# Seven products of quarters for the second layer of the late slots in a gated cross-attention and mixture-of-experts kernel

## The chip, the core and the metric

The kernel runs on one core of one Trainium2 chip. The metric is the device time of one execution in microseconds. Everything is float32.

## The reference

Four sequences of 1024 tokens with 256 features pass through a gated cross-attention block (16 heads, 64 context tokens for each sequence), and then through a gated feed-forward block of eight experts, of which each token takes two. Cut to what matters here:

```python
x = x + tanh(g_xattn[0]) * xattn(layernorm(x), ctx, ...)

def ffn(x, gate_w, w1, w2):              # x: the layer-normed tokens
    logits = einsum('td,ed->te', xt, gate_w)
    w_topk, sel = top_k(logits, 2)       # 2 of 8 experts, softmax over the two
    combine = zeros(T, E).at[arange(T)[:, None], sel].add(softmax(w_topk))
    h = silu(einsum('td,edf->tef', xt, w1))     # first layer,  256 -> 1024
    y = einsum('tef,efd->ted', h, w2)           # second layer, 1024 -> 256
    return einsum('ted,te->td', y, combine)

x = x + tanh(g_ffn[0]) * ffn(layernorm(x), ...)
```

The kernel doesn't compute all eight experts for each token. It sorts (token, expert) pairs by expert and multiplies only those.

## The kernel before

**Attention** runs over eight groups of 512 tokens. Its parts (queries, scores at L385, softmax, `attend`, `project`) are issued in an order written out by hand in the loop over `g`. While it runs, the routing of the finished groups is worked out on VectorE (`route`, `place`), and lists of (token, weight) pairs are written to memory.

**Slots.** The expert layers run over slots. A slot is one expert and 256 places of its list, in two blocks of 128 tokens. There are 9 early slots (`NA`), taken from the first half of the tokens, and late slots from `s = NA` on. The first seven late slots (9 to 15, `NW`) are wide: they have a third block of 128 tokens. The next five (16 to 20, `NH`) have a third block of 64 tokens. The others (21 to 27) are short and have two blocks. Slot 27 (`s = NA + OFTEN - 1`) is the last that always runs; more slots lie behind a branch.

For each slot:

- `load_ids` and `load_weights` load the list entries and the expert's w1 and w2 on SP's queue, three slots ahead.
- `gather_tokens` fetches the normed tokens with GpSimd's indirect DMAs (L845); `transposed` transposes them on TensorE (L867), and ScalarE copies them out of PSUM.
- `hidden` is the first layer: TensorE at L899, and ScalarE's Silu out of PSUM into `hT` at L907.
- `combine` is the second layer. It gathers the tokens' present outputs into `acc` (GpSimd, L922). For each block `t` it multiplies `hT` by `w2` over 8 tiles of the hidden dimension (TensorE, L978: the stationary operand is a 128x128 tile of `hT`, the moving one 256 columns of w2). Then `add(t)` follows: VectorE takes the product out of PSUM, times each token's weight (L966), into `y` (the tile that held the gathered tokens), GpSimd adds `y` to `acc` (L970), and a scatter writes `acc` back (L939).

`run_slots` puts `combine(s)` behind `hidden(s + 1)` and the transposes of slot `s + 2`, so that TensorE always has work while the other engines finish. Only at the end does the combine of slot 26 follow directly on that of slot 25, ahead of `hidden(27)`. A gather into `acc` waits for the scatters of the slot before it, since both go over the same rows of the output.

**Buffers.** PSUM: the pool `ps1` has four banks, which queries, transposes, and the second layer share in the order in which they come free; the hidden layer has the pool `ps2`. `hT` has two buffers in the share `hidden`, or lies in `group`. The tag `pr` (two buffers) and the tag `nT` (four) are large tiles of the attention phase; in the late slots, `nT` also holds the transposed tokens of wide slots.

The scheduler of the language orders the instructions of each engine; `keep_in_program_order` and `issue_after` pin some of them. Each engine runs its own instructions in that order.

Of the kernel before, what the change touches and what calls it, by code (L numbers as in the profile page):

```python
# [8 lines left out]
F32 = mybir.dt.float32  # L9
I32 = mybir.dt.int32  # L10
AF = mybir.ActivationFunctionType
ALU = mybir.AluOpType
# [3 lines left out]
P = 128  # L16
# [5 lines left out]
def kernel(  # L22
# [13 lines left out]
    w2: bass.AP,  # L36
    out: bass.AP,
):

# [21 lines left out]
    nc = tc.nc  # L61

    B, L, D = x.shape
    M = context.shape[1]
    H, _, DK = w_qs.shape
    E, _, F = w1.shape
# [8 lines left out]
    NF = F // P  # L75
# [5 lines left out]
    NA = -(-(2 * HG * G - E * (S - 1)) // S)  # L81
# [4 lines left out]
    OFTEN, RARELY = 19, 20  # L86
# [27 lines left out]
    of = out.rearrange("b l d -> (b l) d").rearrange("(g t p) d -> g p t d", p=P, t=T)  # L114
# [14 lines left out]
    nT = {}  # L129
# [104 lines left out]
    def apart(tensor, dma, part=None, behind=()):  # L234

        writers = [writer for name in behind for writer in written[name]]
        tc.declare_no_dep(dma.ins, group=tensor, keep=writers, reason="different rows")
        tc.add_to_no_dep_group(tensor, dma.ins)
        for writer in writers:
            tc.add_manual_dep(  # L240
                dma.ins,
                writer.name,
                mybir.DependencyInfo(mybir.DependencyClass.Sync, mybir.DependencyReason.DATA),
                reason="rows of the part",
            )
        if part:
            written.setdefault(part, []).append(dma.ins)
# [133 lines left out]
    def probabilities(g, t, qT):  # L381

        sc = ps2.tile([P, NP // 2, 2, 2, M], F32, tag="ps2", name=f"sc_{g}_{t}")
        for p in range(NP):
            nc.tensor.matmul(  # L385
                sc[:, p // 2, :, p % 2, :],
                of_pair(qT, p)[:, t * P : (t + 1) * P],
                kT[g // GB][:, p, :],
                start=True,
                stop=True,  # L390
            )
        scv = sc.rearrange("p q r j m -> p (q r j) m")
        mx = small.tile([P, H], F32, tag="mx", name=f"mx_{g}_{t}")
        nc.vector.tensor_reduce(mx, scv, AX.X, ALU.max)  # L394
        pr = soft.tile([P, H, M], F32, tag="pr", name=f"pr_{g}_{t}")
        nc.vector.tensor_tensor(  # L396
            pr, scv, mx.unsqueeze(2).to_broadcast([P, H, M]), ALU.subtract
        )
        nc.scalar.activation(pr, pr, AF.Exp)  # L399
        sm = small.tile([P, H], F32, tag="sm", name=f"sm_{g}_{t}")  # L400
        nc.vector.tensor_reduce(sm, pr, AX.X, ALU.add)  # L401
        nc.vector.reciprocal(sm, sm)  # L402
        newest[:] = [
            nc.gpsimd.tensor_tensor(pr, pr, sm.unsqueeze(2).to_broadcast([P, H, M]), ALU.mult).ins  # L404
        ]
        return pr
# [352 lines left out]
    half = len(tiles) // 2  # L759
# [77 lines left out]
    def behind_softmax():  # L837

        return tc.issue_after(newest[0]) if newest else nullcontext()
# [71 lines left out]
    evicted = {}  # L911

    def combine(s, ids, b, y, acc, hT):

        blocks = blocks_of(s)
        n = tokens_of(s)
        behind = [f"slot{s - 1}"] if s else ["out0"]
        if s == NA:
            behind.append("out1")
        for t, r in enumerate(blocks):  # L920
            with behind_softmax():
                gather = nc.gpsimd.indirect_dma_start(  # L922
                    out=acc[t][:r],
                    out_offset=None,
                    in_=outf[:n],
                    in_offset=bass.IndirectOffsetOnAxis(ap=ids[:r, t, 0:1], axis=0),
                    bounds_check=n - 1,
                    oob_is_err=False,
                )
            apart("out", gather, behind=behind)  # L930
        if attention_ends:
            py = [bank(f"py_{s}_{t}")[:, : D * r // P] for t, r in enumerate(blocks)]
        else:
            both = bank(f"py_{s}").rearrange("p (t d) -> p t d", d=D)
            py = [both[:, t, :] for t in range(blocks)]

        def scatter(t):
            r = blocks[t]
            put = nc.gpsimd.indirect_dma_start(  # L939
                out=outf[:n],  # L940
                out_offset=bass.IndirectOffsetOnAxis(ap=ids[:r, t, 0:1], axis=0),
                in_=acc[t][:r],
                in_offset=None,
                bounds_check=n - 1,
                oob_is_err=False,
            )
            apart("out", put, f"slot{s}")

        def parts_of(r):

            return [(slice(i * r, (i + 1) * r), slice(i * D * r // P, (i + 1) * D * r // P)) for i in range(P // r)]

        def add(t):
            r = blocks[t]
            last = s == NA + OFTEN - 1 and t == len(blocks) - 1
            if last:
                tc.keep_in_program_order(
                    nc.vector.scalar_tensor_tensor(
                        acc[t], py[t], ids.bitcast(F32)[:, t, 1:2], acc[t], ALU.mult, ALU.add
                    )  # L960
                )
                scatter(t)
                return

            for rows, columns in parts_of(r):
                evicted[s] = nc.vector.tensor_scalar(  # L966
                    y[t][:r, columns], py[t][rows], ids.bitcast(F32)[rows, t, 1:2], None, ALU.mult
                ).ins
            with behind_softmax():
                nc.gpsimd.tensor_tensor(acc[t][:r], acc[t][:r], y[t][:r], ALU.add)  # L970
                scatter(t)

        each = attention_ends
        per_tile = NF // len(hT)
        for t, r in enumerate(blocks):
            for f in range(NF):
                for rows, columns in parts_of(r):
                    nc.tensor.matmul(  # L978
                        py[t][rows],
                        hT[f // per_tile][:, f % per_tile, t * P : t * P + r],  # L980
                        b[:, f, columns],
                        start=(f == 0),
                        stop=(f == NF - 1),
                    )
            if each:
                add(t)
            yield
        if not each:
            for t in range(len(blocks)):
                add(t)  # L990
# [3 lines left out]
    def run_slots(slots):  # L994
# [28 lines left out]
        for s in slots:  # L1023
            gather(s + ahead)
            a, b = weights.pop(s)
            xin, acc = tokens.pop(s)
            if s == slots[-1] and pending:
                yield from combine(*pending)
                pending = None
            for hT in hidden(s, a, xT):  # L1030
                yield
            if s + 1 in slots:
                xT = transposed(s + 1, tokens[s + 1][0])
                yield
# [74 lines left out]
    for g in range(NG + 3):  # L1109
# [9 lines left out]
        for t in range(T):  # L1119
            if g < NG:  # L1120
                pr = probabilities(g, t, qT)
# [93 lines left out]
```

## Time and profile before

| | |
|---|---|
| median of 3 runs | 889.73 us (889.43 to 890.48) |
| profiled execution, own time | 918.12 us |
| its span, first to last instruction | 916.3 us, mean granted TensorE clock 0.986 |
| TensorE matmuls (PE) busy | 871.4 us (95%) |
| weight loads (PEld) busy | 657.5 us (72%) |
| VectorE (DVE) busy | 327.8 us (36%) |
| ScalarE (ACT) busy | 263.9 us (29%) |
| GpSimd (POOL) busy | 403.0 us (44%) |
| second layer, L978: busy, share of the chain that ended last | 238.3 us, 23% |

The profile is of one execution, whose own time is longer than the median of the runs without a profile. A row of the groups' view has the line, the engine, the operation, out <- in by the program's names, partitions x elements, the count, the busy time, the mean time of one, and the idle time before. Matmul records overlap: the next starts before the last has left the array, so that the distance between starts is the cost, and not the mean duration. Each float32 matmul in the code leaves two matmul records and two weight loads. In the timeline a row merges equal instructions that follow each other: start, length, engine, line, operation and count.

### The profile page before, as it was taken

How to read it: one execution, taken by the hardware profiler on the slowest of the kernel's cores; microseconds unless marked ns; L12 is line 12 of the kernel's file. 1: busy time of each engine (PE TensorE's matmuls, PEld its weight loads, DVE VectorE, ACT ScalarE, POOL GpSimd, SP SyncE). 2: the span in 40 equal slices, each digit the busy share in tenths (PEclk: the TensorE clock that was granted, in tenths of full speed). 3: DMA queues.
4: the chain of work that ended last, by engine and by line, in shares of the span. 5: the costliest groups of instructions: out<-in, count | busy, mean ns of one | idle time of the engine just before them, and what ended most of it. 6: DMA issues, size and time to landing. Idle time of an engine off the chain costs nothing.

```text
span 916.3 us, 11723 instructions
## 1 busy us (share of the span) xinstructions
PE 871.4 (95%) x4328; PEld 657.5 (72%) x4328; DVE 327.8 (36%) x729; ACT 263.9 (29%) x414; POOL 403.0 (44%) x392
## 2 busy tenths in 40 slices
PE   8999999999999998997997899999999999999995
PEld 5556858574857576865885787777777777888884
DVE  3467585777468748631155300000000001100010
ACT  4653353425242425432140121211211211121110
POOL 2051212146213553065447565555455555564443
PEclk9999999999999999998998899999999999999998
DMA  9600000001010225276372575744444564457111
GB/s 203 195 1 1 24 24 24 24 19 30 1 46 1 47 90 188 72 141 143 115 262 63 143 248 166 237 149 140 148 140 142 176 198 148 135 188 267 51 36 42
DMA packets 85279, 102.33 MB, mean 112 GB/s; under 512 B 29366, under 2 KB 71740, under 8 KB 85216
## 3 DMA queue, kind: packets, MB, share of 16 engines
q1 hardware_dynamic: 62656, 66.96, 24.4%
q0 software_dynamic: 11600, 25.25, 8.8%
q10 hardware_dynamic: 10960, 9.31, 3.7%
q8 instruction: 36, 0.59, 0.3%
q14 instruction: 27, 0.22, 0.1%
HBM read 84.75 MB, written 17.33 MB: 111 GB/s over the span
## 4 chain that ended last, share of the span: by engine, by line
PE 80%; DVE 10%; another core or an unknown queue 3%; issue 3%; DMA 1%; POOL 1%; ACT 1%; POOLq 0%; ACTq 0%; DVEq 0%
PE py L978 23%; PE ph L899 22%; PE pp L445 11%; PE pq L370 10%; PE sc L385 5%; PE pa L414 2%; PE pt L867 2%; PE po L428 2%; DVE qT L437 1%; PE pk L317 1%; DVE sm L401 1%; DVE pr L396 1%; DVE mx L394 1%; PE pt_b L281 1%
## 5 line engine op out<-in xcount | busy, mean ns | idle before, releaser
L978 PE MATMUL py<-w,hT 128*128 128x256 f32 (+1 forms) x1168 | 238.3, 369 | 9.2 <-issue 8.7
L899 PE MATMUL ph<-xT,w 128*128 128x256 f32 (+2 forms) x896 | 233.8, 418 | 2.1 <-ACT xT L872 1.2
L978 PEld LDWEIGHTS py<-w,hT 128*128 128x128 f32 (+1 forms) x1168 | 199.8, 184 | 40.2 <-issue 14.0
L899 PEld LDWEIGHTS ph<-xT,w 128*128 128x128 f32 x896 | 170.0, 191 | 57.5 <-issue 1.6
L907 ACT ACTIVATE hT<-ph 128x1024 f32<-128x1024 f32 (+3 forms) x84 | 69.9, 835 | 370.6 <-PE ph L899 319.5
L966 DVE TENSOR_SCALAR x<-py,ids 128x256 f32<-128x256 f32 (+1 forms) x72 | 33.5, 465 | 381.9 <-PE py L978 348.3
L404 POOL TENSOR_TENSOR pr<-pr,sm 128x1024 f32<-128x1024 f32 x32 | 60.9, 1902 | 218.1 <-DVE sm L402 202.1
L370 PE MATMUL pq<-nT_a,wq 128*128 128x512 f32 x256 | 117.0, 597 | 0.4 <-issue 0.2
L445 PE MATMUL pp<-wp,qT 128*128 128x256 f32 x512 | 113.2, 379 | 0.0
L445 PEld LDWEIGHTS pp<-wp,qT 128*128 128x128 f32 x512 | 97.0, 190 | 18.2 <-issue 5.3
L922 POOL DMA_INDIRECT x<-out_dram,ids x68 | 69.3, 1018 | 81.7 <-DMA out_dram<-x,ids 61.9
L845 POOL DMA_INDIRECT x<-normed,ids x68 | 67.9, 999 | 53.4 <-DMA ids<-lists 34.3
L970 POOL TENSOR_TENSOR x<-x,x 128x256 f32<-128x256 f32 (+1 forms) x67 | 48.3, 721 | 90.5 <-DVE x L966 77.8
L370 PEld LDWEIGHTS pq<-nT_a,wq 128*128 128x128 f32 x256 | 45.9, 190 | 53.5 <-issue 47.6
L939 POOL DMA_INDIRECT out_dram<-x,ids x68 | 69.0, 1015 | 23.2 <-POOL x L970 18.0
L568 POOL DMA_INDIRECT lists<-entry,to_row x64 | 62.1, 971 | 20.5 <-issue 17.9
L385 PEld LDWEIGHTS sc<-keys,qT 128*128 128x128 f32 x512 | 62.9, 192 | 7.9 <-issue 7.5
L385 PE MATMUL sc<-keys,qT 128*128 128x128 f32 x512 | 67.4, 278 | 0.0
L415 ACT COPY aT<-pa 128x512 f32<-128x512 f32 x64 | 34.6, 590 | 91.2 <-PE pa L414 71.1
L394 DVE TENSOR_REDUCE mx<-sc 128x16 f32<-128x1024 f32 x32 | 39.0, 1220 | 29.5 <-PE sc L385 28.3
L401 DVE TENSOR_REDUCE sm<-pr 128x16 f32<-128x1024 f32 x32 | 38.9, 1215 | 20.9 <-ACT pr L399 20.9
L377 ACT COPY qT<-pq 128x512 f32<-128x512 f32 x64 | 35.7, 582 | 28.4 <-PE pq L370 28.4
(209 smaller groups left out, 624.8 us busy)
## 6 DMA issues: line engine op xcount, KB each, us to landing
w<-in_L_ffn_w_dram SPq DMA_DIRECT2D x56, 1024.0 KB
out_dram<-x ACTq DMA_DIRECT2D x8, 512.0 KB
normed<-keep_b ACTq DMA_DIRECT2D x8, 512.0 KB
x<-in_x_dram SPq DMA_DIRECT2D x7, 512.0 KB
x<-normed,ids POOLq DMA_INDIRECT x68
x<-out_dram,ids POOLq DMA_INDIRECT x68
out_dram<-x,ids POOLq DMA_INDIRECT x68
wq<-in_L_xattn_w_qs_dram SPq DMA_DIRECT2D x4, 256.0 KB
```

The costliest lines, as they stand in the source:

```text
L370: nc.tensor.matmul(pq, wq[:, c, p * P : (p + 1) * P], nT[g][:, c, :], start=(c == 0), stop=(c == NC - 1),)
L385: nc.tensor.matmul(sc[:, p // 2, :, p % 2, :], of_pair(qT, p)[:, t * P : (t + 1) * P], kT[g // GB][:, p, :], start=True, stop=True,)
L404: nc.gpsimd.tensor_tensor(pr, pr, sm.unsqueeze(2).to_broadcast([P, H, M]), ALU.mult).ins
L445: nc.tensor.matmul(pp[:, i, :], of_pair(qT, p)[:, t * P : (t + 1) * P], wp[:, p, :], start=(p == 0), stop=(p == NP - 1),)
L568: nc.gpsimd.indirect_dma_start(out=lists, out_offset=bass.IndirectOffsetOnAxis(ap=to_row[:, k, i : i + 1], axis=0), in_=entry[:, k, i, :], ...
L845: gather = nc.gpsimd.indirect_dma_start(out=xin[t][:n], out_offset=None, in_=normed[: tokens_of(s)], in_offset=bass.IndirectOffsetOnAxis(a ...
L899: nc.tensor.matmul(ph[:, i, :], a[:, c, f * P : (f + 1) * P], xT[:, c, :], start=(c == 0), stop=(c == NC - 1),)
L907: nc.scalar.activation(hT[f0 // per_tile][:, f1 : f1 + step, :], ph, AF.Silu)
L922: gather = nc.gpsimd.indirect_dma_start(out=acc[t][:r], out_offset=None, in_=outf[:n], in_offset=bass.IndirectOffsetOnAxis(ap=ids[:r, t, 0 ...
L939: put = nc.gpsimd.indirect_dma_start(out=outf[:n], out_offset=bass.IndirectOffsetOnAxis(ap=ids[:r, t, 0:1], axis=0), in_=acc[t][:r], in_of ...
L970: nc.gpsimd.tensor_tensor(acc[t][:r], acc[t][:r], y[t][:r], ALU.add)
L978: nc.tensor.matmul(py[t][rows], hT[f // per_tile][:, f % per_tile, t * P : t * P + r], b[:, f, columns], start=(f == 0), stop=(f == NF - 1),)
```

## The change

For the late slots 9 to 26, the second layer of the two whole blocks is computed as one matrix product of 256 tokens x 1024 hidden by 1024 hidden x 256 outputs, cut in the middle along all three. That makes four quarters of `hT`, four of `w2` and four of the output. The output's quarters come from seven products of quarters (in place of eight), of which five use sums of quarters:

- `quarters()` lets VectorE form eight sums of 128 partitions x 512 elements: s1 to s4 of `hT`'s quarters and t1 to t4 of `w2`'s. s3 is written over a quarter of `hT` and t1 over a quarter of `w2`; the others go to tiles of the tags `pr` and `nT`.
- `seven_products()` has TensorE multiply 128x128 tiles, four for each product, each product into a PSUM bank of its own. ScalarE takes product 1 out twice (once for each block's weights, into `partial`), and VectorE adds each of the others to the quarters of `y` in which it takes part, times the token's weight: eight `scalar_tensor_tensor` of 128x128. `finish(i)` is the add to `acc` and the scatter of block `i`.
- A third block, where there is one, is multiplied as before, but now ahead of the two whole blocks. Its `add`, which VectorE begins by taking it out of PSUM, is issued behind `quarters()`.

The early slots, slot 27 and the slots behind the branch stay as they are.

In the built program the scheduler moves some of VectorE's sums: s1 of the next slot stands among the additions of the slot before, and t3 (in short slots t1 too) of the next slot ahead of them. t1, t2 and t4 of wide slots stand directly ahead of the third block's leave from PSUM; in slots with a half block the leave's two halves stand on either side of t4. On GpSimd, the third block's add and scatter go ahead of those of the two whole blocks. ScalarE gets two more instructions a slot, and SP's order is unchanged.

```diff
+        whole = 2 if NA <= s < NA + OFTEN - 1 else 0
         if attention_ends:
-            py = [bank(f"py_{s}_{t}")[:, : D * r // P] for t, r in enumerate(blocks)]
+            py = [bank(f"py_{s}_{t}")[:, : D * r // P] if t >= whole else None for t, r in enumerate(blocks)]
...
+        def quarters():
...
+            s1, s2, s3, s4 = sums[:, 0], sums[:, 1], h[1][0], rest[:, 0]
+            t1, t2, t3, t4 = w[0][1], more[:, 0], rest[:, 1], more[:, 1]
+            for to, one, sign, other in (
+                (s1, h[1][0], ALU.add, h[1][1]),
+                (s3, h[0][0], ALU.subtract, h[1][0]),
+                (s2, s1, ALU.subtract, h[0][0]),
+                (s4, h[0][1], ALU.subtract, s2),
+                (t3, w[1][1], ALU.subtract, w[0][1]),
+                (t1, w[0][1], ALU.subtract, w[0][0]),
+                (t2, w[1][1], ALU.subtract, t1),
+                (t4, w[1][0], ALU.subtract, t2),
+            ):
+                nc.vector.tensor_tensor(to, one, other, sign)
+            return h, w, (s1, s2, s3, s4), (t1, t2, t3, t4)
+
+        def seven_products(h, w, hsums, wsums):
...
+            def product(name, left, right):
+                to = bank(f"py_{s}_{name}")[:, :P]
+                n = NF // 2
+                for f in range(n):
+                    nc.tensor.matmul(to, left[:, f, :], right[:, f, :], start=(f == 0), stop=(f == n - 1))
+                return to
...
+            def plus(to, of, i, sofar):
+                evicted[s] = nc.vector.scalar_tensor_tensor(to, of, weight[i], sofar, ALU.mult, ALU.add).ins
+
+            p = product("1", h[0][0], w[0][0])
+            for i in range(2):
+                nc.scalar.activation(partial[:, i], p, AF.Copy, scale=weight[i])
+            p = product("2", h[0][1], w[1][0])
+            plus(own[0], p, 0, partial[:, 0])
+            fifth = product("5", s1, t1)
+            plus(own[1], fifth, 0, partial[:, 0])
+            p = product("7", s3, t3)
+            plus(own[2], p, 1, partial[:, 1])
+            p = product("6", s2, t2)
+            plus(own[1], p, 0, own[1])
+            plus(own[2], p, 1, own[2])
+            plus(own[3], fifth, 1, own[2])
+            p = product("3", s4, w[1][1])
+            plus(own[1], p, 0, own[1])
+            finish(0)
+            p = product("4", h[1][1], t4)
+            plus(own[2], p, 1, own[2])
+            finish(1)
+
+        def finish(i):
+            with behind_softmax():
+                nc.gpsimd.tensor_tensor(acc[i], acc[i], y[i], ALU.add)
+                scatter(i)
+
         each = attention_ends
         per_tile = NF // len(hT)
         for t, r in enumerate(blocks):
+            if t < whole:
+                continue
             for f in range(NF):
...
-            if each:
+            if each and not whole:
                 add(t)
             yield
+        if whole:
+            operands = quarters()
+            for t in range(whole, len(blocks)):
+                add(t)
+            seven_products(*operands)
+            yield
```

More of the change, by code (lines that the diff above doesn't have):

```diff
@@ L971, in add @@
                 scatter(t)
+        def quarters():
+            half = NF // 2
+            if len(hT) == 2:
+                h = [[hT[k][:, :, i * P : (i + 1) * P] for k in range(2)] for i in range(2)]
+            else:
+                h = [
+                    [hT[0][:, k * half : (k + 1) * half, i * P : (i + 1) * P] for k in range(2)]
+                    for i in range(2)
+                ]
+            w = [[b[:, k * half : (k + 1) * half, j * P : (j + 1) * P] for j in range(2)] for k in range(2)]
+            sums, more = (
+                soft.tile([P, 2, half, P], F32, tag="pr", name=f"{kind}_{s}") for kind in ("hsum", "wsum")
+            )
+            rest = npool.tile([P, 2, half, P], F32, tag="nT", name=f"rest_{s}")
+            s1, s2, s3, s4 = sums[:, 0], sums[:, 1], h[1][0], rest[:, 0]
[12 more added lines that the diff above has]
+            return h, w, (s1, s2, s3, s4), (t1, t2, t3, t4)
@@ new lines, in seven_products @@
+        def seven_products(h, w, hsums, wsums):
+            s1, s2, s3, s4 = hsums
+            t1, t2, t3, t4 = wsums
+            weight = [ids.bitcast(F32)[:, i, 1:2] for i in range(2)]
+            def product(name, left, right):
[4 more added lines that the diff above has]
+                return to
+            partial = work.tile([P, 2, P], F32, tag="xn", name=f"partial_{s}")
+            own = [y[i][:, j * P : (j + 1) * P] for i in range(2) for j in range(2)]
+            def plus(to, of, i, sofar):
[19 more added lines that the diff above has]
+            finish(1)
```

## The prediction

> **What bounds the kernel now.** I read the page first: span, shares, the 40 slices and the granted clock.
>
> ```profile
> span 916.3 us, 11723 instructions
> PE 871.4 (95%) x4328; PEld 657.5 (72%) x4328; DVE 327.8 (36%) x729; ACT 263.9 (29%) x414; POOL 403.0 (44%) x392
> ...
> PE   8999999999999998997997899999999999999995
> ...
> DVE  3467585777468748631155300000000001100010
> ...
> PEclk9999999999999999998998899999999999999998
> ```
>
> TensorE (PE) is full in nearly every slice. From slice 24 on (about 550 us), where the late slots run, its digits are 9 and VectorE (DVE) stands at 0 or 1. The windows view gives PE 385.06 of 386.00 us busy between 520 and 906 us at clock 1.00. So what shortens a late slot on PE shortens the kernel, and VectorE has some 90% of its time free there.
>
> Then the timeline, because overlapping records make a mean duration useless as a cost; a cost on PE is the distance between starts.
>
> ```profile
> 628.42 10.53 PE L978 MATMUL py<-w,hT 128*128 128x256 f32 x48
> 638.79 10.48 PE L899 MATMUL ph<-xT,w 128*128 128x384 f32 x32
> 649.11 0.82 PE L867 MATMUL pt<-ident,x 128*128 128x128 f32 x6
> 649.76 2.54 PE L978 MATMUL py<-w,hT 128*128 128x256 f32 x11
> ```
>
> This is one wide slot (three blocks). 48 records in 638.79 - 628.42 = 10.37 us: 216 ns each, without a gap. (Each float32 matmul of the code leaves two records; all counts of matmuls below are of records.) A block is 16 of them, 3.46 us; the two whole blocks that the change touches are 32 x 216 ns = 6.91 us.
>
> The new products are 128 columns wide with 128x128 weights changed at every matmul. The attention scores, L385, have just that shape:
>
> ```profile
> 249.83 1.03 PE L445 MATMUL pp<-wp,qT 128*128 128x256 f32 x4
> 250.69 1.95 PE L385 MATMUL sc<-keys,qT 128*128 128x128 f32 x16
> 252.47 1.04 PE L414 MATMUL pa<-ident,pr 128*128 128x128 f32 x8
> ```
>
> 16 in 252.47 - 250.69 = 1.78 us: 111.5 ns each, 3.5 over half of 216. For VectorE's sums the near rows are the routing's, plain 128x512 float32 operations; the last two have both operands in SBUF, as the sums have:
>
> ```profile
> 181.72 0.68 DVE L490 TENSOR_TENSOR cmp<-lg 128x512 f32<-128x512 f32 x1
> 182.32 0.68 DVE L491 TENSOR_TENSOR cmp<-lg 128x512 f32<-128x512 f32 x1
> ...
> 183.05 0.68 DVE L492 TENSOR_TENSOR cmp<-cmp,before 128x512 f32<-128x512 f32 x1
> ...
> 184.78 0.68 DVE L493 TENSOR_TENSOR cmp<-cmp 128x512 f32<-128x512 f32 x1
> ```
>
> 0.68 us each; the next starts after 0.60 us if it doesn't need the result (L490 to L491), and after 0.73 if it does (L491's start to L492's).
>
> **The change, part by part.** It touches 18 slots (9 to 26): seven wide ones, five with a half block ("half"), six short ones.
>
> *PE.* 32 records of 256 columns go, 7 x 4 x 2 = 56 of 128 columns come: 56 x 111.5 ns = 6.24 us for 6.91, so -0.66 us a slot and -11.9 us over 18, if nothing stalls. One product is 0.89 us. A rule speaks against this. The Trainium skill, "TensorE: Matmul & The Clock Gate", section "Back-to-back issue gap", says that in a stream of weight loads and matmuls both set the spacing, and gives 81 ns at 128 columns where the column count alone would give 56. By that ratio (estimate) the 128-column pitch here would be 108 x 81/56 = 156 ns, a slot +1.83 us and the kernel +33 us. The L385 row has the same weights, shape and type, and shows 111.5; I take the row. Break-even is 122 ns. The first matmul of each product carries a wait; blocks of L978 start with one today, and the pitch across it is the same 216.
>
> *VectorE: eight sums a slot.* 8 x 0.60 to 0.73, some 5.3 us. Short slots: they start when the slot before has left PSUM, 0.8 us into the next hidden stage, which occupies PE 6.9 us, plus 0.4 of transposes; product 5, the first to need a sum, is 1.8 us further. They are ready 3 us early. Without that cover up to 5.3 us a slot would show. Only slot 26 has none (its combine follows slot 25's directly), but there both sums of w2 that write t3 and t1 and the first of hT stand ahead of slot 25's last steps; product 7 needs s3 at about 7.5 us after slot 25's products start, and comes up at 8.9. I cost it at 0. The weights that the sums read are loaded three slots ahead, tens of us before.
>
> *The wait in wide slots.* The third block now comes first. t1 is written in place into w2, which the third block's matmuls read, so VectorE stops at t1 until they end (T0), and t2, t4 and the block's leave from PSUM queue behind it. Hand-over PE to DVE: the last record ends 0.16 us after its pitch, and 0.04 more (638.95 to 638.99, L966). t1 0.20 to 0.89, t2 0.93 to 1.62, t4 1.66 to 2.35, the leave (0.48, L966) 2.27 to 2.75. PE meanwhile does products 1, 2 and 5 (5 needs t1, ready at 0.95, comes up at 1.78). Product 7 takes the third block's PSUM bank: it would start at 2.68 and can at 2.81, +0.13 us. Behind the leave VectorE has eight additions of 128x128: between the 0.35 of L966's 64x128 form and the 0.48 of 128x256, taken as 0.35, since that form has the same 128 columns. Product 3 takes product 2's bank, free at 3.1, due at 4.6; product 4 takes product 7's, free at 4.4, due at 5.5. No more stall. Seven slots x 0.13 = +0.9 us.
>
> *Half slots.* The same queue, but product 6 takes that bank, due 3.57; the leave ends at about 2.8. 0.
>
> *ScalarE.* Two scaled copies of 128x128 a slot, new: 0.27 each by the slope of its copies (0.425 us for 320 columns, 0.58 for 512), at most 0.43. Ready by 1.9 us; first read behind the leave, and needed by PE only for product 6's or 7's bank. 0.
>
> *GpSimd and its DMAs.* Same number of adds, gathers and scatters, in another order: the third block's add and scatter first, the two others together at the end. The last scatter of a wide slot starts some 1.2 us later after the slot's start. Gathers behind it:
>
> ```profile
> 640.56 0.99 POOL L939 DMA_INDIRECT out_dram<-x,ids  x1 [0.28 <-POOL x L970]
> 643.83 1.05 POOL L922 DMA_INDIRECT x<-out_dram,ids  x1 [2.28 <-DMA out_dram<-x,ids]
> ...
> 650.42 0.94 POOL L845 DMA_INDIRECT x<-normed,ids  x1 [0.31 <-issue]
> ```
>
> Six in a row, ending 1.6 us into the next combine (649.76). Later by 1.2 plus the 0.5 that the slot is shorter, they end 3.3 us into it, just under T0 (3.46), and the next add waits for the leave at T0 + 2.75. Covered by 3 us. SP issues the same loads in the same order. 0.
>
> *The end.* The last scatter starts at 907.26, behind PE's last block (L958 ends 906.98). The last accumulator gathers wait for slot 26's scatters; by the same steps they land about 0.9 us ahead of that block's end. So PE still sets the end, with little to spare. 0, bounded at +1.
>
> Sum: -11.9 + 0.9 = **-11.0 us**. Against the profiled execution: 918.1 (span 916.3, 1.8 around it) to 907.1. That execution stands 28.4 over the median of the three runs; its half-clock stretches all lie ahead of 502 us but for the tail, and the late stage ran at clock 1.00, so I take the same difference off the median: 889.7 - 11.0 = **878.7 us**.
>
> **The rivals.**
>
> *The port (slower).* GpSimd's work gets between t1, t2, t4 and the leave. The Trainium skill, "SBUF — State Buffer", section "Who interferes with whom", says that a VectorE instruction with two SBUF inputs contends with a GpSimd instruction that reads SBUF[...]. No late VectorE instruction of today has two SBUF inputs; all eight sums have. For: GpSimd is busy 54% of that stage, its gathers end just at T0, and its adds (0.72 us) fall on the sums behind the products and may push them further. Against: the routing's L492 and L493 show no stretch, but GpSimd was idle beside them. Price: each of the three sums up to 1.0 us late (a gather's length), the leave up to d = 3 late. A wide slot is then at -0.53 + d, a half one at -0.66 + (d - 0.8), the six short ones together at -4. It decides from d = 1.25 us; d = 2 gives +9 (899), d = 3 gives +21 (911). Without the rule d is 0.
>
> *A part of that.* d of 0.3 to 1 in most wide slots, or the additions nearer to 0.48 and PE catching the wait for product 4: half of the gain goes, about 885.
>
> *The weight load binds.* 156 ns a record: 923. Only if the L385 row were not typical.
>
> *Nothing changes.* The end goes over to the chain of scatters and gathers, or the losses happen to cancel: 889.7. The change does do what it says: 56 narrow for 32 wide is in the built program.
>
> **How the numbers follow.** Forecast 0.63, own range 875 (a pitch of 109, as L414's transposes have, gives another -2.5) to 883. Part of the port 0.15. The port in full 0.15, weight load 0.03, nothing 0.04. Less than 0.2% (1.8 us) can't be told from no change here. Faster 0.78, same 0.04, slower 0.18. Range 875 to 893: it leaves out the upper part of the slower case and a gain of over 15.
>
> **What would show it.** Right: records of the product line 111 to 112 ns apart; a wide slot 0.5 us shorter (21.3 to 20.8), a short one 14.3 to 13.6; one PE gap of about 0.13 us before product 7 of wide slots, behind the leave; sums of 0.68 us. Wrong: a pitch of 120 or over; PE gaps over 1 us before product 7 (the leave late); sums of over 1 us beside a gather or an add (the port); or PE waiting at the very end for a gather.

## Result: what was measured, and the profile after

| | before | after |
|---|---|---|
| median, us | 889.61 (889.43 to 890.48, 4 runs) | 878.16 (877.45 to 879.09, 4 runs) |
| ratio | | 0.987, 95% interval 0.9855 to 0.9884 |
| profiled execution, us | 918.12 | 877.45 |

The kernel became 11.45 us faster; 11.0 was predicted. The profiled execution of before was a long one, and its extra 28 us lie ahead of the late slots, where its granted clock was 0.94 (400 to 460 us) and 0.87 (460 to 512 us; it stayed low until 511, not 502 as I had read it). Slot 9's products start at 586.18 us there, at 556.60 after (not counting two records that stand ahead of slot 10's hidden stage in both). So the stage itself is compared, from there to the start of slot 27's last record: 319.90 us before, 308.43 after, -11.47. That is the whole difference of the medians. Ahead of the stage the profiled runs e1 and e3 (before with small edits) start slot 9 at 558.33 and 557.98 us, e2 and e4 (after with small edits) at 558.07 and 556.83, so no gain shows there.

The page of after, its span, its shares and three rows of its 40 slices:

```profile
span 875.5 us, 12972 instructions
...
PE 849.5 (97%) x4760; PEld 658.0 (75%) x4760; DVE 459.4 (52%) x981; ACT 274.4 (31%) x450; POOL 415.0 (47%) x392
...
PE   7999999999999999899999999999999999999995
...
DVE  3466485687558675763138301543344455556560
...
PEclk9999999999999999999999999999999999999998
```

VectorE's digits in the last third went from 0 and 1 to 3 to 6: that is the sums and the eight additions out of PSUM. TensorE's did not move: it is as full as before, of shorter work. One wide slot (12) on TensorE, from the timeline (start, duration, engine, line, tiles, shape, count):

```profile
618.22 3.62 PE L1063 MATMUL py<-w,hT 128*128 128x256 f32 x16
621.67 1.95 PE L1021 MATMUL py<-w,hT 128*128 128x128 f32 x16
623.46 1.06 PE L1021 MATMUL py<-w,hsum 128*128 128x128 f32 x8
624.35 1.06 PE L1021 MATMUL py<-rest,hT 128*128 128x128 f32 x8
...
627.92 4.36 PE L902 MATMUL ph<-xT,w 128*128 128x384 f32 x13
```

First the third block (L1063), then products 1 and 2 in one row of 16, 5 (`w,hsum`), 7 (`rest,hT`), and at 627.92 the next hidden stage. From 621.67 to 627.92 there are 56 records in 6.25 us, 111.6 ns each, with nothing between them.

Taken by kinds of slot, from the distance between the first products of neighbouring slots:

| slots | before, us each | after, us each | sum | predicted |
|---|---|---|---|---|
| 7 wide (9 to 15) | 21.34 (three of them; 20.16 to 21.78) | 20.68 (19.51 to 21.11) | -4.59 | -3.7 |
| 5 half (16 to 20) | 18.80, 18.80, 18.16, 16.35, 16.35 | 17.95, 17.95, 17.40, 15.69, 15.60 | -3.87 | -3.3 |
| 4 short (21 to 24) | 14.25 | 13.60 | -2.60 | -2.6 |
| 2 short (25 and 26 in one) | 20.72 | 20.31 | -0.41 | -1.3 |

The predicted column is the recorded sum shared out: -0.66 a slot, and +0.13 in each wide one.

### The profile page after: what moved, and what is told of

Read it like the earlier page. It is cut to its first block, busy times and chain, and to the rows that moved or that the text cites. A ratio compares the mean times of both kernels' runs of the same rounds, so it can differ in the third digit from the quotient of the medians.

```text
span 875.5 us, 12972 instructions
## 1 busy us (share of the span) xinstructions
PE 849.5 (97%) x4760; PEld 658.0 (75%) x4760; DVE 459.4 (52%) x981; ACT 274.4 (31%) x450; POOL 415.0 (47%) x392
## 4 chain that ended last, share of the span: by engine, by line
PE 83%; DVE 11%; issue 2%; DMA 1%; ACT 1%; POOL 1%; DVEq 0%; ACTq 0%; POOLq 0%
PE ph L902 24%; PE py L1021 12%; PE pp L448 11%; PE py L1063 11%; PE pq L373 10%; PE sc L388 5%; PE pa L417 2%; PE po L431 2%; PE pt L870 2%; DVE qT L440 1%; DVE sm L404 1%; PE pk L320 1%; DVE pr L399 1%; DVE mx L397 1%; PE pt_b L284 1%
## 5 line engine op out<-in xcount | busy, mean ns | idle before, releaser
L902 PEld LDWEIGHTS ph<-xT,w 128*128 128x128 f32 x896 | 168.2, 190 | 54.4 <-ACT xT L875 1.4
L925 POOL DMA_INDIRECT x<-out_dram,ids x68 | 72.0, 1059 | 82.7 <-DMA out_dram<-x,ids 59.7
L1063 PE MATMUL py<-w,hT 128*128 128x256 f32 (+1 forms) x592 | 106.5, 352 | 0.0
L1063 PEld LDWEIGHTS py<-w,hT 128*128 128x128 f32 (+1 forms) x592 | 89.5, 176 | 11.2 <-issue 0.3
L848 POOL DMA_INDIRECT x<-normed,ids x68 | 70.7, 1039 | 48.6 <-DMA ids<-lists 29.0
L943 POOL DMA_INDIRECT out_dram<-x,ids x68 | 73.5, 1080 | 22.4 <-POOL x L1053 9.8
L1004 DVE TENSOR_TENSOR w<-w 128x512 f32<-128x512 f32 x18 | 12.7, 708 | 92.5 <-PE py L1063 92.3
L970 DVE TENSOR_SCALAR x<-py,ids 128x256 f32<-128x256 f32 (+1 forms) x36 | 15.9, 443 | 79.1 <-PE py L1063 78.9
L455 DVE SCALAR_TENSOR_TENSOR x<-pp,tg,x 128x512 f32<-128x512 f32 x16 | 12.0, 750 | 66.8 <-PE pp L448 66.8
```

Of the source, the lines that this page charges most:

```text
L848: gather = nc.gpsimd.indirect_dma_start(out=xin[t][:n], out_offset=None, in_=normed[: tokens_of(s)], in_offset=bass.IndirectOffsetOnAxis(a ...
L902: nc.tensor.matmul(ph[:, i, :], a[:, c, f * P : (f + 1) * P], xT[:, c, :], start=(c == 0), stop=(c == NC - 1),)
L925: gather = nc.gpsimd.indirect_dma_start(out=acc[t][:r], out_offset=None, in_=outf[:n], in_offset=bass.IndirectOffsetOnAxis(ap=ids[:r, t, 0 ...
L943: put = nc.gpsimd.indirect_dma_start(out=outf[:n], out_offset=bass.IndirectOffsetOnAxis(ap=ids[:r, t, 0:1], axis=0), in_=acc[t][:r], in_of ...
L1063: nc.tensor.matmul(py[t][rows], hT[f // per_tile][:, f % per_tile, t * P : t * P + r], b[:, f, columns], start=(f == 0), stop=(f == NF - 1),)
```

## Experiments

A "period" below is the distance between the first products of neighbouring slots in the profiled run; "the stage" is the one from slot 9 to slot 27. The runs e5 to e8 were measured in one round, in which the kernel before took 914.86 us (902.39 to 927.15), though the record names the same chip for all runs. That spread is wider than the gain, so their traces are read by stage. In e5, e7 and e8 some half slots were also longer than in after, by up to 1.4 us; the wide and short slots of e7 and e8 were not. In e6, e7 and e8 TensorE stood in some of these slots ahead of product 7, in e7 and e8 by up to 0.8 us, behind ScalarE's copies of product 1; why the copies came late is open.

**e1_third_first.** The kernel before, with only the order of the blocks changed:

```diff
-        for t, r in enumerate(blocks):
+        turn = list(enumerate(blocks))
+        if NA <= s < NA + OFTEN - 1:
+            turn = turn[2:] + turn[:2]
+        for t, r in turn:
```

> The kernel before, with one edit: in the late slots 9 to 26 the third block is multiplied ahead of the two whole blocks; the products stay as they were. If the gain is TensorE's columns alone, this is worth next to nothing: only the five slots with a half block may win up to 0.2 us each at the changes of shape (their periods fell by 0.85 us in the changed kernel, against 0.65 elsewhere), so 888.6 to 889.6. If moving the third block ahead is a good part of the gain (its leave from PSUM lies earlier, and so does its add), it shows here: 884 or less.

Measured: 889.17 us, ratio 0.9996 (0.9987 to 1.0005). The order alone is worth nothing that a timing can tell. In the trace it gives 0.61 us, all of it in the half slots (18.80 to 18.61 twice, 18.16 to 18.05, 16.35 to 16.25 once). A half slot on TensorE:

```profile
742.55 9.07 PE L981 MATMUL py<-w,hT 128*64 128x128 f32 x64
751.46 8.78 PE L899 MATMUL ph<-xT,w 128*128 128x320 f32 x32
```

The 64 records (32 of the half block, then 32 of 256 columns; the row names the first form) take 8.91 us from start to start. With the half block last they took 9.00, and the hidden stage behind them 8.72 up to its transposes, where this one takes 8.61. So with the half block last such a slot takes some 0.1 us more at two places, next to the records of 64-column weights; why is not shown. The rest of the gain, over 10 us, is left for the products.

**e3_eight_narrow.** The kernel before with its blocks cut into halves of 128 columns, so eight products' worth of columns at the new shape:

```diff
-            for f in range(NF):
+            narrow = NA <= s < NA + OFTEN - 1 and t < 2
+            sides = [slice(0, P), slice(P, D)] if narrow else [None]
+            for f, side in [(f, side) for side in sides for f in range(NF)]:
...
+                    columns = side or columns
...
-                        py[t][rows],
+                        py[t][rows, side] if side else py[t][rows],
```

> The kernel before, with one edit: in the slots 9 to 26 the two whole blocks are multiplied in 128 columns at a time, all columns with new weights: 64 records of 128 columns in place of 32 of 256. If a narrow record costs 111.7 ns wherever it stands, a slot takes 64 x 111.7 - 32 x 216 = +0.24 us and the kernel +4.3 us: 893.9. If narrow records are bound by their weight loads when they follow each other for long, it is more (at 122 ns +16 us). If the gain has nothing to do with the number of columns, this is at or below 889.6.

Measured: 894.42 us, ratio 1.0048 (1.0031 to 1.0065). A short slot on TensorE:

```profile
840.01 7.31 PE L981 MATMUL py<-w,hT 128*128 128x128 f32 x64
847.15 7.07 PE L899 MATMUL ph<-xT,w 128*128 128x256 f32 x32
```

That is 4.8 us over before, where 4.3 was expected; the stage is 4.5 longer. 64 records in 847.15 - 840.01 = 7.14 us are 111.6 ns each, where 32 of 256 columns take 6.91. Halving the columns costs 0.23 us for a pair of blocks; leaving out one product of the eight is worth 7.14/8 = 0.89.

**e7_short_eight.** After, with eight products in the short slots:

```diff
-        whole = 2 if NA <= s < NA + OFTEN - 1 else 0
+        whole = 2 if NA <= s < NA + NW + NH else 0
```

> The kernel after with seven products in the wide and half slots only (9 to 20); the six short slots (21 to 26) have eight products, as in the kernel before. Theory: a short slot goes back from 13.60 to 14.25 us, slots 25 and 26 from 20.31 to 20.72: 5 periods, +0.65 x 4 + 0.41 = +3.0 us, about 881.2, and the wide and half periods stay at 20.68 and 17.95. If the gain came from the wide and half slots' order alone, 0; if it were all from the number of slots changed, 6/18 of 11.5 = +3.8.

Measured: 911.70 us in the round named above, which as a time says nothing. In the trace, at a granted clock of 1.00, the short periods are back at 14.25 (four times) and 20.72, together +3.01 as expected, and the wide ones stay at 20.68. The gain goes slot by slot with the products.

**e2_no_sums.** After, without VectorE's eight sums: the seven products take plain quarters in their place (the sums are left out, the products stay, and the output is not the reference's).

```diff
-            for to, one, sign, other in (
...
-                nc.vector.tensor_tensor(to, one, other, sign)
+            s1, s2, s3, s4 = h[1][0], h[1][1], h[0][0], h[0][1]
+            t1, t2, t3, t4 = w[0][1], w[1][1], w[1][0], w[0][0]
```

> The changed kernel without VectorE's eight sums; the seven products take single quarters in their place, so the output is not the reference's. If the sums are hidden but for slot 26, where product 6 and product 3 came 0.31 and 0.41 us late, it saves 0.7 us: 877.5. If they cost something in each slot (a later start of products, slower gathers beside them), it saves more: at 0.3 us a slot, 873.

Measured: 878.25 us, ratio 0.9869 (0.9851 to 0.9887), the same as after. All periods of wide, half and the first four short slots are as in after to 0.01 us: there the sums are free. Only slots 25 and 26 went from 20.31 to 19.42. I had expected that 0.7 of it would show in the time, and it did not; e10 returns to this.

**e4_leave_first.** After, with the third block's leave written ahead of the sums in the program.

```diff
         if whole:
-            operands = quarters()
             for t in range(whole, len(blocks)):
...
+            operands = quarters()
```

> The changed kernel with the third block's leave from PSUM issued ahead of the sums in place of behind them. t1 waits for only half of the third block (it started 1.5 us before the block's end), so the leave behind the sums was ready 1.7 us ahead of product 7. If so, the order is free: 878.2 within 0.3, although t1, t2, t4 then stand behind the leave and come 0.5 to 2 us later (product 5 needs t1 1.8 us after the third block, product 6 t2 3.6 us after). If the place of the sums is worth something, the twelve slots with a third block move by 0.1 us or more each: 877 or 879.5.

Measured: 878.63 us, ratio 0.9873 (0.9856 to 0.9889). The trace shows `t1`, `t2`, `t4` still ahead of the leave (620.38, 621.10, 621.83, leave 622.44): the scheduler kept its order. The run is a repeat of after (stage 308.41) and says nothing about the order.

**e5_sums_twice.** After, with each sum issued twice, the copy to a place that is written again:

```diff
+                if to is s3:
+                    again = s4
+                elif to is t1:
+                    again = t2
+                else:
+                    again = to
+                nc.vector.tensor_tensor(again, one, other, sign)
                 nc.vector.tensor_tensor(to, one, other, sign)
```

> The kernel after, with each of VectorE's eight sums issued twice (the copy goes to a place that is written again afterwards, so the values stay). It adds 8 x 0.60 to 0.69 us to VectorE in a slot, about 5 us, 90 us over 18 slots, and nothing to TensorE. Theory (hidden, with a known slack): in short slots the last sum that product 5 or 7 needs is ready 8 us before it in the trace of after, so 0. In wide slots the block's leave moves from 622.21 to about 624.3 us, and product 7, which takes its bank, starts at 624.35 with 1.7 us of slack: +2.1 - 1.7 = +0.4 us in seven slots, +3. Half slots 0. Slot 26, which has no cover, +2 to +4. In sum +5 to +7 us, about 884. If the sums were not hidden: +5 us in each of 18 slots, +90 us. If t1 waited for the whole third block, as my prediction had it: +2.1 us in each wide slot, +15 from these alone.

Measured: 915.52 us, ratio 1.0007 (0.9971 to 1.0042) to the kernel before in that round: the whole gain is gone. TensorE lost little of it: the stage is 310.70 us, 2.3 over after, and the wide slots keep 20.68 (the scheduler now put the leave between `t1` and `t2`, so my +0.4 there failed). TensorE's last record starts at 896.48. Three rows of GpSimd, and the first and the last sum that stand beside the first of them:

```profile
807.62 8.83 POOL L925 DMA_INDIRECT x<-out_dram,ids  x1 [0.30 <-issue]
...
851.39 5.94 POOL L1060 TENSOR_TENSOR x<-x,x 128x256 f32<-128x256 f32 x1 [1.60 <-DVE w L1011]
...
906.89 1.00 POOL L943 DMA_INDIRECT out_dram<-x,ids  x1 [0.30 <-issue]
```

```profile
807.12 0.68 DVE L1011 TENSOR_TENSOR hsum<-hT 128x512 f32<-128x512 f32 x1
...
815.66 0.69 DVE L1011 TENSOR_TENSOR rest<-w 128x512 f32<-128x512 f32 x1
```

GpSimd's last scatter starts 10.4 us after TensorE's last record does; in after and in the other three kernels of that round it is 1.2 to 1.4. Each slot's accumulators are gathered behind the scatters of the slot before, and one turn of that chain takes 9.2 us (892.30 to 901.51) when nothing else holds it. It fell behind for the most part in three single instructions: a gather of 8.83 us, one of 3.80 (at 828.35) and an addition of 5.94, where after has at most 1.49 and 1.14. Each of them stood beside sums that followed one another without a pause and kept their 0.68 us (15 of them from 807.12 to 816.35), and ended with the last of these; only the sum at the end of the addition took longer, 1.10. The means of the late stage (gathers of accumulators 1442 ns against 1071 in after, additions of 128x256 912 against 739) come for the most part from these three. All three theories that I wrote down missed this: the sums do not press on TensorE first, but on GpSimd.

**e6_adds_to_vector.** After, with the late slots' accumulator additions on VectorE:

```diff
-                nc.gpsimd.tensor_tensor(acc[t][:r], acc[t][:r], y[t][:r], ALU.add)
+                (nc.vector if whole else nc.gpsimd).tensor_tensor(acc[t][:r], acc[t][:r], y[t][:r], ALU.add)
...
-                nc.gpsimd.tensor_tensor(acc[i], acc[i], y[i], ALU.add)
+                nc.vector.tensor_tensor(acc[i], acc[i], y[i], ALU.add)
```

> The kernel after, with the accumulator's additions of the late slots (128x256, both inputs in SBUF) on VectorE in place of GpSimd. TensorE's work is unchanged. Theory (slot 26's sums were late because GpSimd's additions ran beside them): its longest sum falls from 1.71 us to about 0.7, the period of slots 25 and 26 from 20.31 us to about 19.6, the others stay; time 0 to -0.7 us, 877.5 to 878.2. Rival (gathers and scatters do it): the sums of slot 26 stay at 1.0 to 1.7 us and the period at 20.3. Second rival: VectorE, which takes its instructions in order, now waits for the accumulator's gathers ahead of sums or of additions out of PSUM: products come late in wide slots, +0.5 us or more each, 882 and above.

Measured: 911.69 us, ratio 1.0002 (0.997 to 1.0034) to the kernel before in that round. In the trace the theory holds, and so does the second rival, though in the half slots and not in the wide ones. Slot 26's sums take 0.68 or 0.69 us each and slots 25 and 26 take 19.42, though GpSimd's scatters (1.56 and 1.48 us) still run beside them: so the additions had stretched slot 26's sums, and the scatters do not. But in the half slots the additions wait on VectorE for gathers, and everything behind them waits too. From VectorE's timeline and from TensorE's:

```profile
789.88 0.42 DVE L974 TENSOR_TENSOR x<-x,x 64x256 f32<-64x256 f32 x1 [1.96 <-DMA x<-out_dram,ids]
```

```profile
790.73 1.16 PE L1021 MATMUL py<-w,rest 128*128 128x128 f32 x8 [1.32 <-DVE x L1029]
```

The last three half periods became 18.00, 17.85 and 18.66 where after has 17.40, 15.69 and 15.60 (a part of that the other runs of the round show too: TensorE stood behind ScalarE's copies of product 1). The stage is 313.73 us, 5.3 over after and 6.2 under before; why the time in this round does not show these 6.2 is open.

**e10_last_adds.** Only the two additions of slot 25 on VectorE:

```diff
-                nc.gpsimd.tensor_tensor(acc[i], acc[i], y[i], ALU.add)
+                adder = nc.vector if s == NA + OFTEN - 3 else nc.gpsimd
+                adder.tensor_tensor(acc[i], acc[i], y[i], ALU.add)
```

> The kernel after with the two accumulator additions of slot 25 alone on VectorE. They are the ones that run on GpSimd beside slot 26's sums. Theory (those two additions cost slot 26 its late products): the period of slots 25 and 26 falls from 20.31 to 19.42 us, as in e6_adds_to_vector and e2_no_sums; at the end the last gather of the accumulator now decides and gives back some 0.4 us (in e2_no_sums the last scatter came 309.31 us after the first products of slot 9, against 309.83 in after, where TensorE had gained 0.89): -0.3 to -0.5 us, about 877.8. Rival (TensorE alone sets the end): -0.9. Rival (the additions delay VectorE): 0 or more.

Measured: 879.21 us, ratio 0.9884 (0.9869 to 0.9898). TensorE did what was expected, 19.42 us for slots 25 and 26; the time did not follow. The sum that had been longest took 0.68 us (847.15). GpSimd's end of the same run:

```profile
865.38 0.72 POOL L974 TENSOR_TENSOR x<-x,x 128x256 f32<-128x256 f32 x1 [2.26 <-DMA x<-out_dram,ids]
...
867.72 1.00 POOL L943 DMA_INDIRECT out_dram<-x,ids  x1 [0.30 <-issue]
```

Counted from the start of slot 10's hidden stage, TensorE's last record starts at 317.96 us in this run (318.85 in after), and the last scatter at 321.02 (320.26 in after). The add waited 2.26 us for its gather to land, 0.50 in after and 1.03 in e2. In these runs the end hangs on the landing of the last gathers, and what TensorE gained there was given back; why the landings differ is not shown. "TensorE alone sets the end" falls; my -0.3 to -0.5 was not seen either.

**e8_three_early, e9_early_six, e11_both, e12_all_early.** Seven products in earlier slots too. e8 and e9 are one kernel; e11 adds e10's edit; e12 takes all nine early slots.

```diff
-        whole = 2 if NA <= s < NA + OFTEN - 1 else 0
+        whole = 2 if 6 <= s < NA + OFTEN - 1 else 0      # e8, e9, e11
+        whole = 2 if 0 <= s < NA + OFTEN - 1 else 0      # e12
```

> The kernel after with seven products in three more slots (6 to 8, whole blocks of 128 rows, which run beside the end of the attention and the routing). Theory (TensorE is full there too and the sums find room on VectorE): 3 x -0.66 = -2.0 us, 876.2. Rival (VectorE is busy there: softmax and routing share it, and the sums' buffers are of the kind that the attention uses): the sums come late, a slot loses 1 to 3 us, 880 to 886.

> The same kernel as e8_three_early (seven products in slots 6 to 8 as well), on a chip whose times are not spread as in that run. In that run's trace slot 6 went from one start of its products to the next in 13.81 us, with a piece of the next hidden stage inside, where the eight products of slot 5 took 14.25. Theory: three slots shorter by 0.4 to 0.66 us, -1.3 to -2.0 us against the kernel after, 876.2 to 876.9. Rival (the sums share VectorE and buffers with the routing and the late table): 879 or more.

> e9_early_six and e10_last_adds together: the two touch different stages, so their effects should add up: -1.6 to -2.5 us against after, 875.7 to 876.6.

> The kernel after with seven products in all nine early slots (0 to 8) as well. If TensorE alone counts: 9 x -0.66 = -5.9 us, 872.3. Against it: slots 0 to 4 run beside the attention, whose softmax has VectorE (two to eight tenths busy, 33.3 of 60 us between 430 and 490 us), and the sums use the attention's buffers (the tag of its probabilities), so the sums wait for the softmax or the softmax for the sums. I expect a loss: 880 to 895.

Measured: e8 912.71 us in the round of the long times; e9 878.04, ratio 0.9877 (0.9863 to 0.9891); e11 880.71, 0.9899 (0.9877 to 0.992); e12 887.61, 0.9964 (0.9951 to 0.9977). In e9's profiled run the three slots did bring their share: from the start of slot 7's hidden stage to that of slot 10's it took 45.75 us, 47.73 in after, -1.98 or 3 x 0.66. But from slot 4's to slot 7's it took 50.23 for 44.91: there TensorE waited 3.00 us for VectorE's routing (`chosen`, L502), and from 466 to 478 us it had a granted clock of 0.86. VectorE's rows and TensorE's:

```profile
464.56 0.69 DVE L1004 TENSOR_TENSOR rest<-w 128x512 f32<-128x512 f32 x1 [3.46 <-DMA w<-in_L_ffn_w_dram]
...
465.77 0.68 DVE L1004 TENSOR_TENSOR w<-w 128x512 f32<-128x512 f32 x1
466.37 0.19 DVE L502 TENSOR_SCALAR chosen<-rank 128x64 f32<-128x64 f32 x1
```

```profile
466.70 0.41 PE L535 MATMUL prow<-chosen,earlier 128*128 128x64 f32 x2 [3.00 <-DVE chosen L502]
```

Two sums of slot 6 (`t3` and `t1`) stand ahead of `chosen`, and the first of them waited 3.46 us for slot 6's w2 to land: the new sums do cause that wait. In after, without them, `chosen` ran at 460.11, and TensorE did not wait for it. In e11's profiled run the same two sums stand in the same place, VectorE does not wait for w2, and TensorE not for `chosen`; so what the sums cost here differs from one execution to the next. That run of e9 was the longest of its five (882.54; three lie at 878.0). What the three at 878.0 lost of the 2 us is open. e11 was to add up and did not. e12 lost against after, as expected, at the shared engine:

```profile
494.58 0.67 DVE L1004 TENSOR_TENSOR hsum<-hT 128x512 f32<-128x512 f32 x1
```

```profile
495.39 2.04 PE L1021 MATMUL py<-w,hsum 128*128 128x128 f32 x8 [8.89 <-DVE where_b L740]
```

TensorE stood 8.89 us ahead of product 5. That product needs the sum s1 (`hsum<-hT`), which VectorE came to at 494.58, in the middle of the table of the late slots (`where_b`); `chosen` itself ran at 474.35, against 460.11 in after. The granted clock of the 53 us from 452 us on was 0.90 (1.00 in that stage of after). No version was faster than after by more than the spread of its runs.

## Why the prediction was right, step by step

**PE's products: right.** 56 records x 111.5 ns for 32 x 216 was forecast as -0.66 us; the short periods gave 14.25 to 13.60, -0.65, and the wide ones 21.34 to 20.68. The row of the attention scores was the right one to take (its 1.78 us over 16 records are 111.3 ns, and the break-even pitch is 6.91 us over 56, 123 ns, not 122; neither changes the sum). e3, with 64 such records in 7.14 us, decides it against the 156 ns that I had estimated from the spacing rule of the Trainium skill, "TensorE: Matmul & The Clock Gate", section "Back-to-back issue gap", by which the short slot would have become longer. That holds for this float32 stream, with two records for each matmul.

**The wait in wide slots: mis-sized, +0.9 us predicted, 0 measured.** The step that failed is "VectorE stops at `t1` until they end (T0)". VectorE in slot 12, from its timeline:

```profile
620.14 0.69 DVE L1004 TENSOR_TENSOR w<-w 128x512 f32<-128x512 f32 x1 [9.83 <-PE py L1063]
...
621.60 0.69 DVE L1004 TENSOR_TENSOR wsum<-w,wsum 128x512 f32<-128x512 f32 x1
622.21 0.48 DVE L970 TENSOR_SCALAR x<-py,ids 128x256 f32<-128x256 f32 x1
```

`t1` starts at 620.14, when the third block (618.22 to 621.67) is little over half done. It is written into one half of the hidden dimension's rows of w2, and the block's matmuls run over those rows in order, so it need only wait for the first half of them. The leave is over at 622.69, and product 7, which takes its bank, starts at 624.35 with 1.7 us to spare. The chain that I drew (`t1`, `t2`, `t4`, leave, bank) exists, and starts 1.7 us sooner than I had it. All seven wide slots show it: `t1` starts 1.5 to 2.0 us after the third block does, never at its end.

**Half slots: 0.6 us too little.** I had counted the same -0.66 there. The order that the change brings, the third block first, is itself worth something there, and I had put it at nothing: e1 measured 0.61 us over five slots, and the table has -3.87 where I had -3.3.

**VectorE's sums: hidden, except where I said that there was no cover.** e2 confirms zero for slots 9 to 24. Slot 26 was the exception that I named and costed at 0, having worked out only when s3 is ready for product 7. That product came in time (846.96); the next ones, which need `t2` and PSUM banks behind the later sums, did not, and slots 25 and 26 lost 0.9 of their 1.3 us. Its timeline, all engines:

```profile
846.30 1.71 DVE L1004 TENSOR_TENSOR wsum<-w 128x512 f32<-128x512 f32 x1
...
846.72 0.73 POOL L1053 TENSOR_TENSOR x<-x,x 128x256 f32<-128x256 f32 x1
...
848.16 1.13 PE L1021 MATMUL py<-wsum,hsum 128*128 128x128 f32 x8
...
849.54 1.16 PE L1021 MATMUL py<-w,rest 128*128 128x128 f32 x8 [0.24 <-DVE x L1029]
```

A sum of 0.68 us (`t2`) took 1.71 beside GpSimd's addition. Product 6, which needs it, came 0.31 us late, and product 3 0.41; the second record of each also came late, by 0.07 and 0.10. Together that is the 0.9. It is the port rival, and this is the one slot where it cost TensorE time. e6 and e10 take that addition away and the lateness with it.

**The port as a rival: right about the mechanism, wrong about its reach.** Sums beside GpSimd's additions are longer: in the late stage of after, 22 sums took 0.85 to 1.71 us, each of them beside an addition, and all others 0.67 to 0.74. `s4` (`rest<-hT,hsum`) met an addition in six of 17 cases and took 1.57 to 1.59 us there, 0.69 elsewhere. In five of the seven wide slots the three sums ahead of the leave meet gathers, not additions, and of these two the gather gives way: at 620.99, beside `t2` and `t4`, one took 1.49 us for the next one's 1.01, while the sums stayed at 0.69. In slots 9 and 10 they do meet additions, as here in slot 10:

```profile
580.23 1.46 DVE L1004 TENSOR_TENSOR wsum<-w,wsum 128x512 f32<-128x512 f32 x1
...
580.38 0.75 POOL L1053 TENSOR_TENSOR x<-x,x 128x256 f32<-128x256 f32 x1
```

There the leave was 0.8 us late (slot 10) and about 1.1 (slot 9), and product 7 still found its bank free, because `t1` had started 1.7 us sooner than I had it. So d, the lateness of the leave behind its sums, was 0 in five wide slots and under the 1.25 us from which the rival decides in the other two. The Trainium skill, "SBUF — State Buffer", section "Who interferes with whom", which spoke for this rival, agrees with the trace where a sum meets an addition, in kind. The 1.03 us by which the sum in slot 26 grew are more than the addition's whole 0.73, though the profile's spans on GpSimd are rough.

**The end: right that TensorE had little to spare.** The end of after, from the same timeline as slot 26:

```profile
863.39 0.72 POOL L974 TENSOR_TENSOR x<-x,x 128x256 f32<-128x256 f32 x1 [0.50 <-DMA x<-out_dram,ids]
...
865.67 0.48 DVE L962 SCALAR_TENSOR_TENSOR x<-py,ids,x 128x256 f32<-128x256 f32 x1 [3.19 <-DMA x<-out_dram,ids]
866.43 1.00 POOL L943 DMA_INDIRECT out_dram<-x,ids  x1 [1.01 <-DVEq L1268]
```

The last addition from PSUM (L962) is released by the landing of the last gather, not by TensorE any more (in before it was TensorE, L978). The last scatter starts 1.41 us after TensorE's last record began; 1.18 before. So the end took 0.2 of the gain, inside the bound of +1. A wait for a gather at the very end was among my signs of being wrong; it came, on VectorE, and was worth no more than that.

**The sum.** Predicted -11.9 + 0.9 = -11.0. Measured: -11.9, half slots -0.6, slots 25 and 26 +0.9 (seen as late products), 0 for the wait: -11.6 from these, -11.47 in the stage, +0.2 at the end, -11.45 in the medians. Two errors of nearly a microsecond each, the wait that did not come and the late products that I had not counted, had opposite signs and hid one another. That the number came within half a microsecond is in part luck; that the products carry the gain is not.

## What to carry to other kernels

Where one engine is full and its pitch is the same for the new shape, price a saving in products by that pitch and believe it; then spend the time on what the helping engine's new work disturbs. Here an in-place operand was released slice by slice, so count the wait from the last reader of that slice, not from the end of the reader's loop. Before giving the helper more work, look at the third engine that shares memory with it, and at the chain that it drives: here the sums hardly hurt TensorE, but twice as many of them, one behind another without a pause, held GpSimd's accumulator chain until it was the end of the kernel. And look at what stands behind a new instruction on the helper: in e9 a sum that waited for its weights held up the routing.

## What the runs showed of the hardware that I had not expected

- A VectorE sum with both inputs in SBUF (128x512, 0.68 us alone) took up to 1.71 us beside one GpSimd addition of 0.73. Beside GpSimd's scatters it stayed at 0.69 while the scatters went from 1.02 to 1.56 us (e10); beside gathers the gather took 1.49 us for 1.01.
- GpSimd can stand still as long as such sums follow one another: in e5 a gather took 8.83 us beside 15 sums, and an addition 5.94, while the sums kept their 0.68. So an addition can give way too, and what decides which of the two does is not shown.
- The order of blocks alone is worth up to 0.2 us on TensorE in a half slot (e1), next to the records of 64-column weights, which no row of a single shape shows.
- One turn of scatter, landing, gather, landing, addition took 9.1 to 9.4 us from slot 26 to slot 27 in after, e2, e5 and e10, where it ran without a wait for products, and what TensorE gained at the end (e2, e10) did not shorten the kernel.
